# A four-layer residual stack on one core: where the gates of the third layer and its weighted candidate are made

## The chip, the cores and the metric

The kernel runs as one program on one core of a Trainium2 chip. The time is the device time of one execution in microseconds (us). The core has five engines, each with its own queue of instructions: TensorE (PE in the profile; PEld is its loading of weights), VectorE (DVE), ScalarE (ACT), GpSimd (POOL) and SyncE (SP, which here only issues DMAs). Engines wait for one another through semaphores. Products land in PSUM; everything else is in SBUF or in DRAM.

## The reference

The input is `x` with 32 rows of 256 steps of 256 features, and a condition vector per row. Four layers follow, each added to `x`. The first two are recurrences, the third is a scan, the fourth two matrix products per row.

```python
# layer 0, for each step t
z = sigmoid(x_t @ W_z + h @ U_z + vz); r = sigmoid(x_t @ W_r + h @ U_r + vr)
hh = tanh(x_t @ W + (r * h) @ U + vh); h = (1 - z) * h + z * hh
# layer 1, for each step t
gate = sigmoid(h1 @ Wh.T + z_t @ Wz.T + b); h1 = tanh(h1 * leak + gate * z_t)
# layer 2
f = sigmoid(x @ W_f.T + b_f); i = sigmoid(x @ W_i.T + b_i); s = f + i + EPS
new_info = (i / s) * (x @ W_h.T + b_h)
c = cumsum(log(f / s + EPS)); hidden = cumsum(exp(c[-1] - c_before) * new_info) + exp(c) * h0
# layer 3, with two matrices per row that are made of the condition vector
out = gelu(x @ down_row) @ up_row
```

In the kernel the candidate of layer 2 is `x @ W_h.T + b_h`, and its gates are `f` and `i`.

## The kernel before, in words

Features lie on the 128 partitions in two chunks (`NC` = 2, called `e` or `k`). All of `x` after layer 1 is kept in one SBUF tile, `X2`, of two chunks by 32 rows by 256 steps. The program has two parts.

**The recurrences** (the loop `for t in range(T + 1)`, 256 steps). Layers 0 and 1 run together, layer 1 one step behind. The batch of 32 is the stationary operand of TensorE (32 columns) and the weights stream past it. A weight matrix is cut into four quarters (`Q` = 4), and the four quarters run beside each other in four column strips of the array, 32 columns each, with `tile_position=(0, j * B)`. The helper `product` (its matmuls are line 528 in the profile) issues eight such matmuls: two chunks by four strips. Each fp32 matmul appears in the trace as two records of weight load and matmul. In one step TensorE does, in this order: `w_U_rz` times `hT` (the gates of layer 0), then whatever `products` holds for the step, then `w_l_Wz` (layer 1), `w_U_h` times `rhT`, `w_l_Wh` times `h1T`, and for the next step `w_W_rzh` times `x` (`project`, which in every second pair of steps first starts a new PSUM tile with the biases, `begin`, line 555). ScalarE makes `r` (line 655) and `z` (line 658, into the tile `keep`), the tanh of layer 1 (637), the tanh of layer 0 into `other` (697), layer 1's gate `gt` (706), and two scaled copies (708). VectorE multiplies `rh` in two halves (676), transposes it (604), combines `keep` (680), scans `h` in two halves (594), transposes that, and scans layer 1's `pre`.

`after(done, z_done)` makes the last matmul of the `w_l_Wz` product wait for `z`, so that the wait is already taken when `w_U_h` comes.

Side work is spread over the steps by dictionaries with a step as key (`transfers`, `products`, `moves`, `additions`, `sigmoids`, `sums`), which `due` empties at fixed places of the step. One kind of side work makes the matrices of layer 3 (`ada_weights`, `ada_matrix`, whose sums on VectorE are line 465). The other is the gates of layer 2, because a stretch of 32 steps (`CT`) can be worked on as soon as layer 1 has passed it. `gate_unit` takes one stretch, eight rows (`CB`) and one feature chunk: four matmuls of 128x128 weights by 256 columns (line 93), two for each gate, one per step; two sigmoids (115); a sum and a guard on VectorE (120, 123); three stores to DRAM (128). Six of the eight stretches (`NW_H` = 6) are done so: 48 units of four matmuls are 192 places. Ten of these places are second places in a step that already has one, every other step from 232 to 250 (`sorted(free + list(range(T - 24, T - 4, 2)))`).

**The turns** (the string `TURN`, run 10 times). Eight groups of four rows go through layers 2 and 3 as a pipeline of stages; a turn works on three groups at once at different stages, and `TURN` is the order in which the stages' instructions are issued to all engines. Per group: `fetch` brings the stored gates from DRAM (145); `late_gates` makes the last two stretches (matmuls at line 93 into `ps_g`, sigmoids 752 and 753, sums 759, 762); `candidate` makes `x @ W_h.T` for two rows and one chunk at a time (line 93 into `ps_c`, 512 columns) and `weigh` adds the bias and multiplies with `i` (777); `logs` (785); `sum_logs` (799); `exponents` (805); `exps` (810, 812); `scale_new` (817); `sum_new` (822); `add_first` (826); `add_hidden` adds to `X2` on GpSimd (833); then per row `middle` and `last`, each four matmuls of 128x128 by 256 columns (845), with a Gelu between them (858); `finish` adds `X2` on VectorE (867), stores the row, and loads the two matrices of the row four later (837).

## Time and profile before

| | |
|---|---|
| runs without a profile | 976.98, 979.28, 973.67 us; median 976.98 |
| the profiled execution | 977.23 us, of which the span from first to last instruction is 975.5 |
| mean granted TensorE clock | 0.993 |
| recurrences: first to last layer-1 tanh (line 637) | 21.1 to 758.4 us |
| one step in the middle of them | 2.86 us |
| turns: from there to the end of the span | 217.1 us |
| distance of equal places of neighbouring turns | 24.35 us |

How to read it: PE's busy time is an overlap of pipelined records, so that a full row of nines says little about how much more it could do. The useful readings are the times between starts of instructions that follow each other on one engine, the note in brackets (how long the engine was idle and who ended it), and the chain that ended last. In the recurrences every step has the same shape, so one step's timeline stands for them all; in the turns, one turn does.

### The profile page before, as it was taken

To read this page: it belongs to the slowest core of one execution; us is meant where nothing else is said; L and a number is where in the kernel's file an instruction comes from. 1 tells how busy PE (TensorE), PEld (TensorE's weight loads), DVE (VectorE), ACT (ScalarE), POOL (GpSimd) and SP (SyncE) were. 2 spreads that over 40 slices of the span, in tenths; PEclk is the share of its full clock that TensorE was granted. 3 is DMA by queue.
4 is the path that set the end of the run, shared out by engine and by line. 5 is a ranking of instruction groups with operands and counts; after the bars stand their busy time and mean duration, and the time that the engine had idled before them with its cause. 6 is when DMAs were issued, how large, how long until landed. Compare 5 with 4: busy or idle time off the path is not lost. (4 is left out here: it accounts for less than half of the span.)

```text
span 975.5 us, 54416 instructions
## 1 busy us (share of the span) xinstructions
PE 934.7 (96%) x22710; PEld 637.3 (65%) x22710; DVE 790.8 (81%) x3409; ACT 557.2 (57%) x2137; POOL 230.2 (24%) x594
## 2 busy tenths in 40 slices
PE   7999999999999999999999999999998889999978
PEld 3666666666666666666666666666665557777756
DVE  4766678888888888888888888888776599999995
ACT  3454455555555555555555555555554688888873
POOL 1233322222222222222222222222222022222222
PEclk9999999999999999999999999999999899999999
DMA  8245212222222222222222122222214747777643
GB/s 279 78 123 150 76 53 77 77 65 95 64 85 83 77 76 69 90 69 90 65 72 87 64 90 64 90 70 74 74 53 122 210 112 228 226 227 227 195 148 144
DMA packets 103577, 107.66 MB, mean 110 GB/s; under 512 B 9089, under 2 KB 86177, under 8 KB 103330
## 3 DMA queue, kind: packets, MB, share of 16 engines
q1 hardware_dynamic: 103330, 104.18, 34.1%
q8 instruction: 178, 2.92, 1.3%
q14 instruction: 69, 0.57, 0.2%
HBM read 59.06 MB, written 45.09 MB: 107 GB/s over the span
## 5 line engine op out<-in xcount | busy, mean ns | idle before, releaser
L528 PE MATMUL p<-w_W_rzh,xT 128*32 128x192 f32 x4096 | 216.3, 327 | 0.1
L594 DVE TENSOR_TENSOR_SCAN h<-other,keep 128x64 f32<-128x64 f32 x512 | 121.3, 279 | 75.2 <-ACT other L697 71.4
L528 PE MATMUL p<-w_U_rz,hT 128*32 128x128 f32 x4080 | 166.0, 279 | 10.5 <-issue 1.7
L697 ACT ACTIVATE other<-p 128x64 f32<-128x64 f32 x256 | 60.0, 234 | 196.4 <-PE p L528 196.4
L701 POOL TENSOR_TENSOR pairs<-xT,hT 128x64 f32<-128x64 f32 x256 | 82.3, 321 | 339.4 <-DVE other L717 280.8
L528 PEld LDWEIGHTS p<-w_U_rz,hT 128*32 128x32 f32 x4080 | 97.9, 108 | 93.5 <-DVE hT L604 90.6
L594 DVE TENSOR_TENSOR_SCAN pre<-other,pairs 128x128 f32<-128x128 f32 x256 | 123.3, 482 | 34.1 <-POOL pairs L701 0.2
L640 POOL TENSOR_TENSOR X<-pairs,h1T 128x64 f32<-128x64 f32 x256 | 96.6, 377 | 230.3 <-DVE rhT L604 226.9
L655 ACT ACTIVATE r<-p 128x64 f32<-128x64 f32 x255 | 57.0, 224 | 158.8 <-PE p L528 158.7
L528 PEld LDWEIGHTS p<-w_W_rzh,xT 128*32 128x32 f32 x4096 | 125.0, 110 | 23.1 <-issue 2.4
L708 ACT ACTIVATE pairs<-h1T,leak 128x32 f32<-128x32 f32 x510 | 133.7, 314 | 0.5
L528 PEld LDWEIGHTS p<-w_l_Wz,pairs 128*32 128x32 f32 x4096 | 77.3, 110 | 86.0 <-issue 70.9
L528 PE MATMUL p<-w_l_Wz,pairs 128*32 128x64 f32 x4096 | 119.6, 225 | 4.2 <-ACT keep L658 1.5
L528 PE MATMUL p<-w_U_h,rhT 128*32 128x64 f32 x4080 | 109.6, 225 | 2.0
L676 DVE TENSOR_TENSOR rh<-r,h 128x32 f32<-128x32 f32 x510 | 75.1, 189 | 41.2 <-ACT r L655 9.0
L528 PE MATMUL p<-w_l_Wh,h1T 128*32 128x64 f32 x4080 | 104.8, 220 | 0.5 <-issue 0.3
L604 DVE STREAM_TRANSPOSE hT<-h 128x32 f32<-128x32 f32 x512 | 84.2, 198 | 0.0
L833 POOL TENSOR_TENSOR X<-X,w 128x512 f32<-128x512 f32 x32 | 41.4, 1307 | 164.7 <-DVE w L826 76.8
L604 DVE STREAM_TRANSPOSE rhT<-rh 128x32 f32<-128x32 f32 x510 | 80.1, 195 | 0.0
L528 PEld LDWEIGHTS p<-w_l_Wh,h1T 128*32 128x32 f32 x4080 | 76.4, 110 | 0.5 <-ACT h1T L637 0.3
L528 PEld LDWEIGHTS p<-w_U_h,rhT 128*32 128x32 f32 x4080 | 69.1, 108 | 8.5 <-DVE rhT L604 8.5
L637 ACT ACTIVATE h1T<-pre 128x64 f32<-128x64 f32 x256 | 67.0, 262 | 1.4 <-DVE pre L594 1.4
(104 smaller groups left out, 1469.0 us busy)
## 6 DMA issues: line engine op xcount, KB each, us to landing
adapted<-wm SPq DMA_DIRECT2D x128, 128.0 KB
wt<-adapted SPq DMA_DIRECT2D x32, 512.0 KB
xT<-in_xT_dram SPq DMA_DIRECT2D x32, 256.0 KB
w<-in_W_dram SPq DMA_DIRECT2D x32, 256.0 KB
out_dram<-y SPq DMA_DIRECT2D x32, 256.0 KB
gates<-gate_i SPq DMA_DIRECT2D x48, 128.0 KB
gates<-gate_s SPq DMA_DIRECT2D x48, 128.0 KB
gates<-gate_g SPq DMA_DIRECT2D x48, 128.0 KB
```

The costliest lines, as they stand in the source:

```text
L528: last = nc.tensor.matmul(ps[j * B : (j + 1) * B, cols], hT[:, k, :], w[:, k, j, :], start=False, stop=False, skip_group_check=True, tile_ ...
L594: nc.vector.tensor_tensor_scan(*(x[:, ns].rearrange("p n u -> p (n u)") for x in (done, other, pairs)), 0.0, ALU.mult, ALU.add,)
L604: nc.vector.transpose(dst[:, c], src[:, bass.ts(c, B)])
L637: nc.scalar.activation(flat(h1T), pre, AF.Tanh)
L640: return nc.gpsimd.tensor_add(X2[:, :, :, s], by_chunk(pairs1.pop(s)[:, :, 0]), h1s.pop(s))
L655: nc.scalar.activation(r, p_0[t][:, cols_0(t, 0, 0)], AF.Sigmoid)
L676: rh_done = nc.vector.tensor_mul(rh[:, cs], r[:, cs], h[:, cs])
L697: nc.scalar.activation(other[:, :, 1], p_0[t][:, cols_0(t, 2, 2)], AF.Tanh)
L701: nc.gpsimd.tensor_add(by_chunk(pairs1[t][:, :, 0]), x_of(t), hT)
L708: nc.scalar.activation(by_chunk(pairs1[s][:, :, 1])[:, c], h1T[:, c], AF.Copy, scale=leak[:, c : c + 1],)
L833: after(nc.gpsimd.tensor_add(x, x, ws[g][:, b]), on_vector)
```

## The change

- **Units.** A unit of `gate_unit` now makes `f`, `i` and the candidate, each in one step: eight matmuls of 128x32 weights by 256 columns, in the four column strips, instead of two of 128x128 in two steps. Three PSUM results alternate between the two halves of `pg`. The candidate's bias and product with `i` (`weigh`) follow on VectorE one step later; `i` is stored after that. Seven stretches (`NW_H` = 7) are made so: 56 units of three places are 168 steps. There are no second places any more.
- **In the steps with such a place** (168; 147 of them where `changed` holds, all but those with `t % 8 == 2`) `w_l_Wz` comes behind `w_l_Wh`, and `gt` behind the two scaled copies. `after(done, z_done)` then puts the wait for `z` on the last of the eight new matmuls.
- **Halves.** `r` and the tanh of layer 0 are each made by two ACTIVATEs of 32 columns.
- **The turns.** `late_gates` makes one stretch with three products (128 columns each); `candidate` is gone; `weigh` has two instructions of 128 columns per group instead of four of 512. `add_hidden` is on VectorE. For three rows of four `X2` is added by TensorE (a matmul with the identity per chunk) and ScalarE copies `y` out. `TURN` has another order; `ps_l` has six buffers instead of four.
- **Transfers.** The matrices of the first four rows are loaded in halves from step 208 on, and the gates of group 0 in six pieces from step 238 on, instead of all after the last step. Chunks of `W2` and the matrices share one pool. The PSUM of the start has a pool of its own that is closed before the loop.

```diff
-NW_H = 6
+NW_H = 7
@@ gate_unit
-        def multiply(name, w, k):
-            gate_product(banks[name], w, e, k, slice(q * CB, (q + 1) * CB), h, h + 1)
+        def multiply(name, w, bank):
+            t["ps" + name] = bank
+            for k in range(NC):
+                for j in range(Q):
+                    js = slice(j * SQ, (j + 1) * SQ)
+                    done = nc.tensor.matmul(
+                        bank[js].rearrange("p (b t) -> p b t", t=CT),
+                        w[:, k, e * P + js.start : e * P + js.stop],
+                        X2[:, k, q * CB : (q + 1) * CB, h * CT : (h + 1) * CT],
...
+                        tile_position=(0, j * SQ),
+                    )
+            return done
+        def weigh():
+            nc.vector.scalar_tensor_tensor(
+                t["i"], t["psc"], vec("b_c", e), t["i"], ALU.add, ALU.mult
+            )
@@ the plan of the steps
-        free = sorted(free + list(range(T - 24, T - 4, 2)))
...
+                    for name, w in (("f", w_f), ("i", w_i), ("c", w_n)):
+                        t = free.pop(0)
+                        at(products, t, multiply, name, w, pg[:, len(units) % 2])
+                        units.add(t)
...
+        for n, (row, m) in enumerate((row, m) for row in range(GB) for m in range(2)):
+            at(transfers, T - 48 + 2 * n, load_matrices, row, slice(m, m + 1))
+        for n, (i, e) in enumerate((i, e) for i in (2, 0, 1) for e in range(NC)):
+            at(transfers, min(stored[0] + 2 + 2 * n, T), fetch_chunk, 0, i, e)
@@ the step
+        def by_halves(dst, src, function):
+            for c in range(NC):
+                nc.scalar.activation(dst[:, bass.ts(c, B)], src[:, bass.ts(c, B)], function)
...
-                        nc.scalar.activation(r, p_0[t][:, cols_0(t, 0, 0)], AF.Sigmoid)
+                        by_halves(r, p_0[t][:, cols_0(t, 0, 0)], AF.Sigmoid)
...
-                due(products, t)
+                done = due(products, t)
+                changed = t in units and t % U1 != U1_0
+                done = done[-1] if t in units else None
...
-                    done = product(p_1[s], cols_1(s), by_chunk(pairs1[s][:, :, 0]), w_1z)
+                    if not changed:
+                        done = with_wz()
                     if run0:
                         after(done, z_done)
...
                     product(p_1[s], cols_1(s), h1T, w_1h)
+                    if changed:
+                        with_wz()
...
-                    nc.scalar.activation(other[:, :, 1], p_0[t][:, cols_0(t, 2, 2)], AF.Tanh)
+                    by_halves(other[:, :, 1], p_0[t][:, cols_0(t, 2, 2)], AF.Tanh)
@@ the turns
+        for gate, w in enumerate((w_f, w_i, w_n)):
             for k in range(NC):
-                gate_product(ps[:, gate], w, e, k, slice(g * GB, (g + 1) * GB), NW_H, NH)
+                gate_product(ps[:, gate], w, e, k, slice(g * GB, (g + 1) * GB), NW_H)
...
+    BY_TENSOR = (1, 2, 3)
     def add_hidden(g, b):
-        after(nc.gpsimd.tensor_add(x, x, ws[g][:, b]), on_vector)
+        return nc.vector.tensor_add(x, x, ws[g][:, b])
...
+            if plus is not None:
+                nc.tensor.matmul(ps[:, e, :], ident, plus[:, e, :], start=False, stop=True)
...
+        if b in BY_TENSOR:
+            nc.scalar.copy(y, ys.pop(row))
```

The order of a turn after the change:

```
mid:1 new:2 new:3 sum:1.1 cum:3 cum:2 sum:0.1 sum:1.0 h0:2.1 sum:0.0 mid:0 h0:2.0
w:1 lf:1 w:0 h0:3.0 x:2 lf:0 last:1 exp:1 h0:3.1 sum:2.0 x:3 last:0 sum:3.1 in:2 y:1
sum:3.0 sum:2.1 exp:0 mid:2 w:3 w:2 ls:1 new:1 ls:0 y:0 cum:1 new:0 lg:1 h0:1.0
mid:3 last:2 h0:1.1 last:3 lg:0 cum:0 exp:3 m:1 x:1 exp:2 y:2 h0:0.1 ln:0 ln:1
h0:0.0 m:0 in:1 x:0 y:3 in:0
```

More of the change, by code (lines that the diff above doesn't have):

```diff
@@ L89, in load_gate_weights, with gate_product @@
         nc.sync.dma_start(out=w, in_=a[name].rearrange("(k p) e -> p k e", p=P))
-    def gate_product(ps, w, e, k, rows, h0, h1):
+    def gate_product(ps, w, e, k, rows, h):
         nc.tensor.matmul(
-            ps[:, 0 : (h1 - h0) * (rows.stop - rows.start) * CT].rearrange(
-                "p (h b t) -> p h b t", h=h1 - h0, t=CT
-            ),
+            ps.rearrange("p (b t) -> p b t", t=CT),
             w[:, k, e * P : (e + 1) * P],
-            X2[:, k, rows, h0 * CT : h1 * CT].rearrange("p b (h t) -> p h b t", t=CT),
+            X2[:, k, rows, h * CT : (h + 1) * CT],
             start=(k == 0),
@@ L101, in gate_product, with gate_unit @@
         )
-    def gate_unit(h, q, e, banks):
+    def gate_unit(h, q, e):
         t = {}
-        def multiply(name, w, k):
-            gate_product(banks[name], w, e, k, slice(q * CB, (q + 1) * CB), h, h + 1)
+        def multiply(name, w, bank):
[7 more added lines that the diff above has]
+                        X2[:, k, q * CB : (q + 1) * CB, h * CT : (h + 1) * CT],
+                        start=(k == 0),
+                        stop=(k == NC - 1),
+                        skip_group_check=True,
+                        tile_position=(0, j * SQ),
+                    )
+            return done
         def unit_tile(name):
@@ L115, in sigmoid @@
             nc.scalar.activation(
-                unit_tile(name), banks[name], AF.Sigmoid, bias=vec("b_" + name, e)
+                unit_tile(name), t["ps" + name], AF.Sigmoid, bias=vec("b_" + name, e)
             )
@@ L125, in guard, with fetch_chunk, fetch, load_matrices @@
             )
+        def weigh():
+            nc.vector.scalar_tensor_tensor(
+                t["i"], t["psc"], vec("b_c", e), t["i"], ALU.add, ALU.mult
+            )
         def store(name):
             nc.sync.dma_start(out=waiting[q][:, "gsi".index(name), e, h], in_=t[name])
-        return multiply, sigmoid, add_up, guard, store
+        return multiply, sigmoid, add_up, guard, weigh, store
     gi = ctx.enter_context(tc.tile_pool(name="gates_in", bufs=1))
     gated = {}
-    def fetch(g, i):
+    def fetch_chunk(g, i, e):
         name = "gsi"[i]
-        pool, bufs = (gp, 2) if i == 2 and g % 3 else (gi, 1)
-        tile_ = gated[name, g] = pool.tile(
-            [P, NC, NH, GB * CT], FP, name=f"in_{name}", tag=f"in_{name}", bufs=bufs
-        )
+        if e == 0:
+            pool, bufs = (gp, 2) if i == 2 and g % 3 else (gi, 1)
+            gated[name, g] = pool.tile(
+                [P, NC, NH, GB * CT], FP, name=f"in_{name}", tag=f"in_{name}", bufs=bufs
+            )
         q, half = divmod(g, CB // GB)
         cols = slice(half * GB * CT, (half + 1) * GB * CT)
+        nc.sync.dma_start(out=gated[name, g][:, e, 0:NW_H], in_=waiting[q][:, i, e, :, cols])
+    def fetch(g, i):
         for e in range(NC):
-            nc.sync.dma_start(out=tile_[:, e, 0:NW_H], in_=waiting[q][:, i, e, :, cols])
+            fetch_chunk(g, i, e)
+    am = ctx.enter_context(tc.tile_pool(name="matrices", bufs=4))
+    matrices = {}
+    def load_matrices(row, ms=slice(0, 2)):
+        if ms.start == 0:
+            matrices[row] = am.tile([P, 2 * NC * D], FP, name="wt", tag="wt").rearrange(
+                "p (m c d) -> p m c d", m=2, d=D
+            )
+        nc.sync.dma_start(
+            out=matrices[row][:, ms].rearrange("p m c d -> p m (c d)"),
+            in_=adapted[row // GB][row % GB, :, ms],
+        )
     with ExitStack() as rec:
@@ L153 @@
         pa = rec.enter_context(tc.tile_pool(name="rec_pa", bufs=2, space=PSUM))
-        px = rec.enter_context(tc.tile_pool(name="aux_ps", bufs=1, space=PSUM))
+        ahead = ExitStack()
+        ph_pool = ahead.enter_context(tc.tile_pool(name="ahead_ps", bufs=1, space=PSUM))
         U0, U1 = 2, 8
@@ L162, in four_banks @@
             return px.tile([P, Q, 512], FP, name=name, tag="px")
-        pg = px.tile([P, 2, CB * CT], FP, name="pg", tag="pg")
         def chunk_tile(name):
-            return ax.tile([P, NC, Q, CH], FP, name=name, tag="w2")
+            return [
+                am.tile([P, Q * CH], FP, name=name, tag="wt").rearrange("p (j n) -> p j n", j=Q)
+                for k in range(NC)
+            ]
         def weights(name, g):
@@ L227 @@
             load_row(a["bias_rows"])
-            w_c = chunk_tile("w_c")[:, :, :, 0 : 3 * S]
+            w_c = [w[:, :, 0 : 3 * S] for w in chunk_tile("w_c")]
             for k in range(NC):
                 nc.sync.dma_start(
-                    out=w_c[:, k], in_=a["C_rzh"][k * P : (k + 1) * P]
+                    out=w_c[k], in_=a["C_rzh"][k * P : (k + 1) * P]
                 )
@@ L293, in rows_into @@
                     )
-            ahead = four_banks("ahead")
-            halves = [ahead[:, half] for half in range(2)]
+            halves = [ph_pool.tile([P, 512], FP, name=f"pv_{half}") for half in range(2)]
             for half in range(2):
                 rows_into(halves[half], 2 * half)
-            pt, ph = (
-                ahead[:, bank, 0 : NC * B].rearrange("p (c b) -> p c b", b=B) for bank in (2, 3)
-            )
+            pt, ph = (ph_pool.tile([P, NC, B], FP, name=name) for name in ("pt", "ph"))
             for k in range(NC):
@@ L313 @@
                             condT[:, k, :],
-                            w_c[:, k, hs, :],
+                            w_c[k][:, hs, :],
                             start=False,
@@ L342 @@
             nc.scalar.preload_act_table_set("sigmoid_and_others")
+            ahead.close()
+        px = rec.enter_context(tc.tile_pool(name="aux_ps", bufs=1, space=PSUM))
+        pg = px.tile([P, 2, CB * CT], FP, name="pg", tag="pg")
         for t, (f, *args) in (
@@ L374, in load @@
                 nc.sync.dma_start(
-                    out=tiles["w2"][:, k, hs],
+                    out=tiles["w2"][k][:, hs],
                     in_=a["W2"][:, k, at_col : at_col + 2 * CH].rearrange(
@@ L395, in multiply @@
                         hyT[:, k, :],
-                        tiles["w2"][:, k, j, :],
+                        tiles["w2"][k][:, j, :],
                         start=(k == 0),
@@ L499 @@
         free = [t for t in range(CT + 3, T) if t not in products]
-        free = sorted(free + list(range(T - 24, T - 4, 2)))
+        units = set()
+        stored = {}
         for h in range(NW_H):
@@ L505 @@
                         free.pop(0)
-                    multiply, sigmoid, add_up, guard, store = gate_unit(
-                        h, q, e, {"f": pg[:, 0], "i": pg[:, 1]}
-                    )
-                    for name, w in (("f", w_f), ("i", w_i)):
-                        for k in range(NC):
-                            t = free.pop(0)
-                            at(products, t, multiply, name, w, k)
-                        at(sigmoids, t, sigmoid, name)
-                    at(sums, t + 1, add_up)
-                    at(sums, t + 2, guard)
-                    for n, name in enumerate("isg"):
-                        at(transfers, t + 2 + n // 2 + (n == 2), store, name)
+                    multiply, sigmoid, add_up, guard, weigh, store = gate_unit(h, q, e)
+                    for name, w in (("f", w_f), ("i", w_i), ("c", w_n)):
+                        t = free.pop(0)
+                        at(products, t, multiply, name, w, pg[:, len(units) % 2])
+                        units.add(t)
+                        if name != "c":
+                            at(sigmoids, t, sigmoid, name)
+                        if name == "i":
+                            at(sums, t + 1, add_up)
+                            at(transfers, t + 2, store, "s")
+                    at(sums, t + 1, weigh)
+                    at(sums, t + 2, guard)
+                    stored[q] = t + 3
+                    for name in "ig":
+                        at(transfers, t + 2 + (name == "g"), store, name)
+        for n, (row, m) in enumerate((row, m) for row in range(GB) for m in range(2)):
+            at(transfers, T - 48 + 2 * n, load_matrices, row, slice(m, m + 1))
+        for n, (i, e) in enumerate((i, e) for i in (2, 0, 1) for e in range(NC)):
+            at(transfers, min(stored[0] + 2 + 2 * n, T), fetch_chunk, 0, i, e)
         assert max(*transfers, *products, *moves, *additions, *sums) <= T
@@ L662, with with_wz @@
                 due(moves, t)
-                due(products, t)
+                done = due(products, t)
+                changed = t in units and t % U1 != U1_0
+                done = done[-1] if t in units else None
+                def with_wz():
+                    return product(p_1[s], cols_1(s), by_chunk(pairs1[s][:, :, 0]), w_1z)
                 if run1:
@@ L705, with gate_1 @@
                     gt = sp.tile([P, S], FP, name="gt", tag="gt")
-                    nc.scalar.activation(gt, p_1[s][:, cols_1(s)], AF.Sigmoid)
+                    def gate_1():
+                        nc.scalar.activation(gt, p_1[s][:, cols_1(s)], AF.Sigmoid)
+                    if not changed:
+                        gate_1()
                     for c in range(NC):
@@ L711 @@
                         )
+                    if changed:
+                        gate_1()
                     if t % U1 == U1_0 and run0:
@@ L718 @@
                     late = s, multiply_add("pre", other, pairs1[s])
-            for g, i in ((0, 2), (0, 0), (0, 1)):
-                fetch(g, i)
             finish_1()
@@ L741 @@
     fs, ss, ccs, ws, pcs, parts_f = {}, {}, {}, {}, {}, {}
-    matrices, mids, ys = {}, {}, {}
-    LATE = slice(NW_H, NH)
+    mids, ys = {}, {}
     def late_gates(g, e):
-        ps = pp.tile([P, 2, 256], FP, name="ps_g", tag="ps_g")
-        for gate, w in enumerate((w_f, w_i)):
+        ps = pp.tile([P, 4, GB * CT], FP, name="ps_g", tag="ps_g")
+        for gate, w in enumerate((w_f, w_i, w_n)):
             for k in range(NC):
-                gate_product(ps[:, gate], w, e, k, slice(g * GB, (g + 1) * GB), NW_H, NH)
-        dst = parts_f[g, e] = gu.tile([P, 256], FP, name="gate_f", tag="gate_f")
+                gate_product(ps[:, gate], w, e, k, slice(g * GB, (g + 1) * GB), NW_H)
+        dst = parts_f[g, e] = gu.tile([P, GB * CT], FP, name="gate_f", tag="gate_f")
+        pcs[g, e] = ps[:, 2]
         nc.scalar.activation(dst, ps[:, 0], AF.Sigmoid, bias=vec("b_f", e))
@@ L755, in late @@
     def late(g, name, e):
-        return gated[name, g][:, e, LATE].rearrange("p h n -> p (h n)")
+        return gated[name, g][:, e, NW_H]
     def late_sum(g, e):
@@ L764, in late_guard, with weigh @@
         )
-    def candidate(g, u):
-        r, e = divmod(u, NC)
-        b0 = g * GB + r * 2
-        ps = pp.tile([P, 512], FP, name="ps_c", tag="ps_c")
-        pcs[g, u] = ps.rearrange("p (h n) -> p h n", h=NH)
-        for k in range(NC):
-            gate_product(ps, w_n, e, k, slice(b0, b0 + 2), 0, NH)
-    def weigh(g, u):
-        r, e = divmod(u, NC)
-        m = gated["i", g][:, e, :, r * 2 * CT : (r + 1) * 2 * CT]
+    def weigh(g, e):
+        m = late(g, "i", e)
         return nc.vector.scalar_tensor_tensor(
-            m, pcs.pop((g, u)), vec("b_c", e), m, ALU.add, ALU.mult
+            m, pcs.pop((g, e)), vec("b_c", e), m, ALU.add, ALU.mult
         )
@@ L828, in add_first, with times @@
         )
+    BY_TENSOR = (1, 2, 3)
     def add_hidden(g, b):
         x = X2[:, :, g * GB + b, :]
-        after(nc.gpsimd.tensor_add(x, x, ws[g][:, b]), on_vector)
-    def load_matrices(row):
-        wt = matrices[row] = ap.tile([P, 2, NC, D], FP, name="wt", tag="wt")
-        nc.sync.dma_start(
-            out=wt.rearrange("p m c d -> p m (c d)"), in_=adapted[row // GB][row % GB]
-        )
-    def times(row, m, src):
-        ps = pp.tile([P, NC, T], FP, name="ps_l3", tag="ps_l3", bufs=4)
+        return nc.vector.tensor_add(x, x, ws[g][:, b])
+    def times(row, m, src, plus=None):
+        ps = pp.tile([P, NC, T], FP, name="ps_l3", tag="ps_l3", bufs=6)
         for e in range(NC):
@@ L849, in times @@
                     start=(k == 0),
-                    stop=(k == NC - 1),
+                    stop=(k == NC - 1 and plus is None),
                 )
+            if plus is not None:
+                nc.tensor.matmul(ps[:, e, :], ident, plus[:, e, :], start=False, stop=True)
         return ps
@@ L861, in last @@
         row = g * GB + b
-        ys[row] = times(row, 1, mids.pop(row))
+        x = X2[:, :, row, :]
+        ys[row] = times(row, 1, mids.pop(row), x if b in BY_TENSOR else None)
     def finish(g, b):
@@ L866, in finish @@
         y = ap.tile([P, NC, T], FP, name="y", tag="y")
-        done = nc.vector.tensor_add(y, ys.pop(row), X2[:, :, row, :])
+        if b in BY_TENSOR:
+            nc.scalar.copy(y, ys.pop(row))
+            done = None
+        else:
+            done = nc.vector.tensor_add(y, ys.pop(row), X2[:, :, row, :])
         nc.sync.dma_start(out=out[:, row], in_=y)
@@ L875 @@
         "lf": (late_gates, 0), "ls": (late_sum, 0), "lg": (late_guard, 0),
-        "c": (candidate, 0), "m": (weigh, 0), "ln": (logs, 0), "in": (fetch, -1),
+        "m": (weigh, 0), "ln": (logs, 0), "in": (fetch, -1),
         "sum": (sum_logs, 1), "w": (exponents, 1), "exp": (exps, 1),
@@ L882 @@
     TURN = """
-        lf:0 new:2 new:3 cum:2 sum:0.0 mid:1 in:2 mid:0 sum:1.0 cum:3 h0:2.0 lf:1 sum:0.1
-        sum:3.1 last:1 sum:1.1 sum:3.0 w:1 exp:1 h0:3.1 h0:2.1 w:0 ls:0 h0:3.0 ls:1 c:0
-        sum:2.0 w:3 lg:0 lg:1 x:2 m:0 y:1 x:3 exp:0 last:0 c:1 m:1 exp:3 c:3 y:0 mid:2 mid:3
-        new:1 sum:2.1 new:0 w:2 cum:0 cum:1 c:2 h0:0.1 h0:0.0 exp:2 ln:1 h0:1.1 h0:1.0 ln:0
-        last:2 x:1 m:3 last:3 y:2 in:1 x:0 m:2 in:0 y:3
+        mid:1 new:2 new:3 sum:1.1 cum:3 cum:2 sum:0.1 sum:1.0 h0:2.1 sum:0.0 mid:0 h0:2.0
[3 more added lines that the diff above has]
+        h0:0.0 m:0 in:1 x:0 y:3 in:0
     """
     with tc.manual_schedule():
-        for row in range(GB):
-            load_matrices(row)
-        tables, on_vector = False, None
+        tables = False
         for turn in range(NG + 2):
@@ L910 @@
                     tables = False
-                on_vector = f(g, *args) or on_vector
+                f(g, *args)
 def _laid_out(v):
```

## The prediction

> **What bounds the kernel now.** I read the page's busy line, then the chain that ended last, then one step's and one turn's timeline.

> ```profile
> PE 934.7 (96%) x22710; PEld 637.3 (65%) x22710; DVE 790.8 (81%) x3409; ACT 557.2 (57%) x2137; POOL 230.2 (24%) x594
> ```

> PE's 96% is an overlap of records and misleads in the recurrences. There a step of 2.86 us is one loop through four engines. From the timeline, the step that begins at 502.91:

> ```profile
> 502.91 0.64 PE L528 MATMUL p<-w_U_rz,hT 128*32 128x128 f32 x16
> ...
> 503.48 0.70 PE L93 MATMUL pg<-X,w_W_f 128*128 128x256 f32 x2
> 503.62 0.22 ACT L655 ACTIVATE r<-p 128x64 f32<-128x64 f32 x1 [0.74 <-PE p L528]
> 503.74 0.22 ACT L658 ACTIVATE keep<-p 128x64 f32<-128x64 f32 x1
> ...
> 503.88 0.29 DVE L676 TENSOR_TENSOR rh<-r,h 128x32 f32<-128x32 f32 x2
> 504.10 0.31 DVE L604 STREAM_TRANSPOSE rhT<-rh 128x32 f32<-128x32 f32 x2
> 504.11 0.27 PEld L528 LDWEIGHTS p<-w_l_Wz,pairs 128*32 128x32 f32 x16 [0.33 <-issue]
> ...
> 504.37 0.27 PEld L528 LDWEIGHTS p<-w_U_h,rhT 128*32 128x32 f32 x16
> ...
> 504.87 0.24 ACT L697 ACTIVATE other<-p 128x64 f32<-128x64 f32 x1 [0.76 <-PE p L528]
> ...
> 505.13 0.47 DVE L594 TENSOR_TENSOR_SCAN h<-other,keep 128x64 f32<-128x64 f32 x2
> ...
> 505.52 0.33 DVE L604 STREAM_TRANSPOSE hT<-h 128x32 f32<-128x32 f32 x2
> ...
> 505.76 0.38 PEld L528 LDWEIGHTS p<-w_U_rz,hT 128*32 128x32 f32 x16 [0.30 <-DVE hT L604]
> ```

> Counted from `w_U_rz`: `r` 0.71, `z` 0.83 to 1.05, `rh` 0.97, `rhT` 1.19, `w_U_h` 1.46, tanh 1.96, scan 2.22, `hT` 2.61, next step 2.86. The gate product ends before `rhT` is there, so it is hidden. Two lines carry the forecast. In a step with little on PE, the last matmul of `w_l_Wz`, which waits for `z`, stands alone 0.5 us after the other seven:

> ```profile
> 62.40 0.26 PEld L528 LDWEIGHTS p<-w_l_Wz,pairs 128*32 128x32 f32 x14 [0.23 <-POOL pairs L701]
> ...
> 62.90 0.14 PEld L528 LDWEIGHTS p<-w_l_Wz,pairs 128*32 128x32 f32 x2 [0.24 <-ACT keep L658]
> ```

> That is 0.05 us after `z` ended. And in the ten doubled steps PE is late:

> ```profile
> 723.39 1.13 PE L93 MATMUL pg<-X,w_W_i 128*128 128x256 f32 x4
> ...
> 724.45 0.43 PE L528 MATMUL p<-w_l_Wz,pairs 128*32 128x64 f32 x16
> 724.64 0.30 PEld L528 LDWEIGHTS p<-w_U_h,rhT 128*32 128x32 f32 x16
> ```

> `w_U_h` starts 1.89 us into the step instead of 1.46, and the step takes 3.26: what PE delays there, the step pays in full.

> In the turns PE and DVE are both full. The windows view and the chain:

> ```profile
> 827.00:852.00 25.00, 25.00 (x98) 18.41 (x98) 24.41 (x43) 22.38 (x32) 5.79 (x6) 1.00 0.73 224
> ```

> ```profile
> 813.42 1.73 PE ps_g L93 x8
> ...
> 837.78 1.73 PE ps_g L93 x8
> ```

> Columns of the first: PE, PEld, DVE, ACT, POOL busy, clock, DMA share, GB/s. A turn is 837.78 - 813.42 = 24.36 us. Start to start, PE needs 16 x 0.216 for `ps_g`, 16 x 0.43 for `ps_c`, 64 x 0.216 for `ps_l`: 24.1. DVE: `cc` 8 x 0.587, `sum_new` 4 x 1.125, `h0` 8 x 0.39, `new` 4 x 0.60, `weigh` 4 x 0.66, `y` and `w` 8 x 0.59, late sums and guards 4 x 0.34: 23.4.

> **The change, part by part.**

> *Gate steps.* Eight column-strip matmuls of 256 columns. Records of 64, 128, 192 and 256 columns take 219, 273, 327 and 379 ns, so a pass streams in 0.21 us, and a strip has four: 0.85 us. Without any wait that ends 0.48 + 0.85 = 1.33 us into the step, before `rhT`: hidden. But the eighth matmul now waits for `z`. `r` in two halves takes ACT 2 x 0.09 us (the 64-column ACTIVATE starts its successor after 0.12, less 0.03 for half the columns) instead of 0.12, so `z` ends at 1.11 and PE sees it at 1.17. Only then may strip 3 begin its second chunk: 0.24 + 0.21, ready at 1.62. `w_U_h` could have started at 1.43 (`rh` 0.03 earlier) and cannot finish in strip 3 before the 1.62 is over. Behind it are queued, on the same strip, `w_U_h`, `w_l_Wh` and now `w_l_Wz` (0.22 each, 504.62 to 504.84), in every second pair of steps `begin` (0.16, 63.72 to 63.88) and `w_W_rzh` (0.65), and ACT waits for all of them. Counted from `r`:

> - through PE alone: `z` seen 0.45, strip 3 done 0.90, three products 1.56, `begin` 1.72, `w_W_rzh` 2.37, `w_U_rz` to `r` 0.67: 3.04 us a step where `begin` stands (86 of the 147 changed steps, counted from the plan);
> - through `hT`, without `begin` (61): 0.90, last group of `w_U_h` to tanh 0.46, to scan 0.23, to `hT` 0.39, to PE 0.24, to `r` 0.71: 2.93 us.

> So 86 x 0.18 + 61 x 0.07 = +20 us. Bounds: below nothing (-0.07 a step if the wait is not felt) and the doubled step's +0.40. I take the walk, which lies nearest to the row at 62.90. The 21 other gate steps keep `w_l_Wz` ahead of `w_U_h`: gate to 1.33, `w_l_Wz` to 1.55, +0.05 each: +1.

> *Halves.* In the 88 steps without a place, `rh` and the scan can start 0.03 us earlier each: 88 x 0.06 = -5; nothing, where VectorE's side sums end just ahead of the scan (they do at 505.13), -6 at most. [...]

> *Doubled steps* gone: 10 x 0.40 = -4.

> *End of the recurrences.* PE idles 1.67 us at 747 while six gate loads run at once, and the granted clock is 0.5 from 749.8 to 753.3. Loads spread over 48 steps may avoid it: -1 (0 to -3). SP only issues them (0.3 us each).

> Recurrences: +20 + 1 - 5 - 4 - 1 = **+11 us**.

> *Turns.* PE: `lf` has 24 records of 128 columns; the 128x32 record with full weights starts its successor after 0.112, so 2.7; `mid` 6.9; `last` 6.9 plus 12 identity records, 2.6: 19.1. DVE loses three `y`, three quarters of `weigh`, 40% of the late sums, and gains four additions at the price of `new`: 4.7 + 4.5 + 3.1 + 2.4 + 0.5 + 0.6 + 2.4 + 0.8 + 2.4 = 21.4. ACT: five table loads of 1.29, `exps` 4 x 1.47, logs 4 x 1.04, Gelu 2.0, sigmoids 1.0, three copies at 0.55: 21.2. DVE and ACT end last now, PE not. The DMA share rises from 0.73 by 7% more bytes in 10% less time to 0.87; a turn's lead covers that. Two full engines that wait for each other will not reach 21.4; PE as the one bound reached 24.36 of 24.1. I take 21.9 (21.4 to 23.5).

> From 788.9 (first `mid`) to 935.0 are six turns: 146.1 - 131.4 = -15. The filling (758.4 to 788.9) loses `ps_c`'s 7 us of PE, but its logs (4.2) and table loads stay: -4 (0 to -7). The last two turns gain 5 us of PE work for the identities and lose three GpSimd additions of 1.3 on the chain: +1 (-2 to +3). Turns: **-18 us**. The first 21 us stay.

> Sum: 977.2 + 11 - 18 = **970 us**, against the profiled execution's own 977.23 (span 975.5 and 1.7 around it); the median, 976.98, is the same within 0.03%.

> **Rivals.**

> - *A: the wait for `z` isn't felt.* If strip 3 catches up, a changed step is 2.86 with `begin` and 2.79 without: -4 in place of +20. 977 - 13 - 18 = 946. For it: the records show strips running independently. Against it: 62.90.
> - *B: the turns don't shorten*, since ACT and DVE hand rows back and forth: 23.5 us a turn, -5 in place of -15: 980. For it: ACT was busy 22.4 of 25 us already. Against it: its work shrinks.
> - *C: slower, by the eighth matmul's wait in the 147 changed steps.* If the late strip also holds back the matmuls dispatched behind it, so that a step costs +0.26 (between the walk's 0.135 and the doubled step's 0.40), that is 38 in place of 20: 988. It decides from +0.22 a step (slower by over 0.5%), and undoes the rest from +0.18.
> - That the change doesn't move the work is excluded: the built order has eight `pg` matmuls per place and no `ps_c`.

> **Numbers.** Half a per cent (4.9 us) is what a measurement of this kernel can tell from no change. Chances: forecast 0.50 (960 to 982; of it 0.36 faster, 0.12 same, 0.02 slower), A 0.20 (faster), B 0.14 (0.10 same, 0.04 slower), C 0.16 (slower). Faster 0.56, same 0.22, slower 0.22. The range takes in A and C: 944 to 988.

> **What would show it.** In a changed step the last two `pg` weight loads stand alone, ended by ACT `keep`, about 1.17 us in; steps of 3.04 and 2.93 in pairs; plain steps at 2.79; no idle PE near the last steps; turns of 21.9 with DVE over 95% busy and PE under 90%. Changed steps at 2.86 or less, or above 3.1, or turns above 23, prove a step wrong.

## The result, and the profile after

The changed kernel took 967.08 us (median of 5 runs, 966.26 to 970.26) against 976.98: a ratio of 0.9905, 95% interval 0.9876 to 0.9934. The forecast was 970. The profiled execution took 968.89 us with a span of 967.1, that is 8.3 us less than the 977.23 of before. The page's busy line, and under it the chain that ended last by engine:

```profile
PE 915.1 (95%) x25046; PEld 700.1 (72%) x25046; DVE 802.8 (83%) x3473; ACT 571.5 (59%) x2682; POOL 195.3 (20%) x562
...
DVE 9%; PE 5%; ACT 3%; DMA 1%; issue 1%; DVEq 0%; ACTq 0%
```

PE has 2336 records of each kind more than before and is busy for less time; as the prediction said, that share decides nothing. Both parts have to be read by their own clocks.

**The recurrences.** The weight loads of a changed step without `begin`, from the timeline (start, duration, engine and line, operation; in brackets the idle time before it and who ended it):

```profile
501.49 0.38 PEld L575 LDWEIGHTS p<-w_U_rz,hT 128*32 128x32 f32 x16 [0.18 <-DVE hT L651]
501.85 0.66 PEld L112 LDWEIGHTS pg<-X,w_W_f 128*32 128x32 f32 x14
502.67 0.14 PEld L112 LDWEIGHTS pg<-X,w_W_f 128*32 128x32 f32 x2 [0.15 <-ACT keep L709]
502.93 0.31 PEld L575 LDWEIGHTS p<-w_U_h,rhT 128*32 128x32 f32 x14
503.13 0.16 PEld L575 LDWEIGHTS p<-w_l_Wh,h1T 128*32 128x32 f32 x4
503.18 0.11 PEld L575 LDWEIGHTS p<-w_U_h,rhT 128*32 128x32 f32 x1
...
503.24 0.11 PEld L575 LDWEIGHTS p<-w_U_h,rhT 128*32 128x32 f32 x1
...
504.41 0.38 PEld L575 LDWEIGHTS p<-w_U_rz,hT 128*32 128x32 f32 x16 [0.18 <-DVE hT L651]
```

Fourteen loads of the gate product run through; the last two, those of the eighth matmul, stand alone at 502.67, 1.18 us into the step, and `keep`, which is `z`, ended their wait. The last two loads of `w_U_h` come at 503.18 and 503.24, after the loads of `w_l_Wh` have begun: what the late strip holds up is its own work, and the other strips go on. The step is 504.41 - 501.49 = 2.92 us long.

To see all steps, I took the distance from one `r` to the next for each of the 254 pairs of neighbouring steps in the trace and sorted them by what the plan puts into the step. "Long" is what all steps together take above the medians of their own kinds (a step under its median counts against it).

| us | plain (86) | gates, `w_l_Wz` ahead (21) | changed, no `begin` (61) | changed, `begin` (86) | long, sum | first to last `r` |
|---|---|---|---|---|---|---|
| before | 2.856 | 2.858 | 2.856 | 2.857 | 9.7 | 735.3 |
| after | 2.801 | 2.886 | 2.918 | 3.036 | 12.0 | 752.6 |

The columns of before are the same steps `t`, whatever they hold there.

**The turns.** One turn in the windows view (us, then busy time of PE, PEld, DVE, ACT, POOL, the granted clock, DMA share, GB/s):

```profile
832.86:854.28 21.42, 19.78 (x100) 17.03 (x100) 21.42 (x41) 21.10 (x33) 0.11 (x1) 1.00 0.88 275
```

VectorE is never idle, ScalarE hardly, and TensorE has 1.6 us left (it is 92% busy, where the prediction asked for under 90%). VectorE's instructions recur every 21.43 us, the Gelus of ScalarE every 21.57; before, a turn took 24.35.

From before to after by these stretches: the first `r` comes at 15.2 us and not at 18.0 (-2.8); the recurrences take 17.3 us more; the rest of the span, 222.2 us before, takes 199.3 (-22.9).

### The profile page after: what moved, and what is told of

It reads as the page before. It is cut to its first block, busy times and chain, and to the rows that moved or that the text cites. A ratio compares the mean times of both kernels' runs of the same rounds, so it can differ in the third digit from the quotient of the medians.

```text
span 967.1 us, 59663 instructions
## 1 busy us (share of the span) xinstructions
PE 915.1 (95%) x25046; PEld 700.1 (72%) x25046; DVE 802.8 (83%) x3473; ACT 571.5 (59%) x2682; POOL 195.3 (20%) x562
## 5 line engine op out<-in xcount | busy, mean ns | idle before, releaser
L659 ACT ACTIVATE other<-p 128x32 f32<-128x32 f32 x512 | 74.7, 200 | 189.9 <-PE p L575 189.9
L659 ACT ACTIVATE r<-p 128x32 f32<-128x32 f32 x510 | 72.8, 195 | 166.8 <-PE p L575 166.8
L575 PE MATMUL p<-w_l_Wz,pairs 128*32 128x64 f32 x4096 | 142.2, 221 | 8.6 <-ACT keep L709 2.8
L575 PEld LDWEIGHTS p<-w_l_Wz,pairs 128*32 128x32 f32 x4096 | 106.0, 110 | 40.0 <-ACT keep L709 12.7
L575 PE MATMUL p<-w_U_h,rhT 128*32 128x64 f32 x4080 | 130.9, 223 | 0.1
L575 PE MATMUL p<-w_l_Wh,h1T 128*32 128x64 f32 x4080 | 126.8, 219 | 1.2 <-ACT other L659 0.6
L575 PEld LDWEIGHTS p<-w_U_h,rhT 128*32 128x32 f32 x4080 | 91.9, 108 | 25.4 <-DVE rhT L651 0.6
L575 PEld LDWEIGHTS p<-w_l_Wh,h1T 128*32 128x32 f32 x4080 | 97.5, 109 | 1.8 <-ACT other L659 0.7
L899 PE MATMUL ps_l<-mid,wt 128*128 128x256 f32 x256 | 66.7, 389 | 12.2 <-ACT mid L914 12.1
L112 PE MATMUL pg<-X,w_W_c 128*32 128x256 f32 x896 | 76.6, 381 | 0.0
```

Source lines behind the costliest of these rows:

```text
L112: done = nc.tensor.matmul(bank[js].rearrange("p (b t) -> p b t", t=CT), w[:, k, e * P + js.start : e * P + js.stop], X2[:, k, q * CB : (q ...
L575: last = nc.tensor.matmul(ps[j * B : (j + 1) * B, cols], hT[:, k, :], w[:, k, j, :], start=False, stop=False, skip_group_check=True, tile_ ...
L659: nc.scalar.activation(dst[:, bass.ts(c, B)], src[:, bass.ts(c, B)], function)
L899: nc.tensor.matmul(ps[:, e, :], matrices[row][:, m, k, e * P : (e + 1) * P], src[:, k, :], start=(k == 0), stop=(k == NC - 1 and plus is N ...
```

## Experiments

Step kinds are written plain / gates with `w_l_Wz` ahead / changed without / changed with `begin`. Times are medians; ratios are to before, run on the same chip. Experiments 1 to 4 ran on one chip, 5 to 8 on a second, 9 to 11 on a third and 12 on a fourth. Steps and long steps are read from the profiled execution.

**1. The wait left off the gate product.**

```diff
-                    if run0:
+                    if run0 and not changed:
                         after(done, z_done)
```

> The early wait for z is no longer put on the eighth gate matmul of the 147 changed steps; the wait then falls on the first w_U_h matmul, which also waits for rhT, so the built order has one more waiting instruction of TensorE's queue there. Theory (the wait holds column strip 3 and with it everything behind it): changed steps fall from 3.04 to about 2.86 where begin stands (86) and from 2.92 to about 2.79 where not (61), -23 us, less what one more waiting instruction after rhT costs (0.06 us a step would give back 9): 944 to 953 us. Rival (TensorE is simply full in these steps, with or without the wait): steps stay at 3.04 and 2.92, 967 us.

998.61 us, ratio 1.0213 (1.0184 to 1.0242): neither side foresaw it. The wait doesn't vanish: `w_U_h` needs `keep`'s semaphore anyhow, and the built program gives it a waiting instruction of its own, for `rhT`, ahead of the matmul that waits for `z` (TensorE has 284 such instructions in this trace, 137 in the changed kernel's). Steps 2.807 / 2.890 / 2.884 / 3.128, so the wait's price did fall in the steps without `begin` (from 2.918). In those with `begin` the step grew from 3.036: in the median `w_U_h` starts 0.78 us after `r` in place of 0.72, and `w_W_rzh`, the last product of the step, 1.54 in place of 1.42. And the long steps rose from 12.0 to 37.2 us. Of TensorE's waits between 25 and 745 us, in the changed kernel and here (line, cause, us in total, times, longest):

```profile
PE p L575 <- issue: 2.9, 7, 0.6
```

```profile
PE p L575 <- issue: 16.0, 34, 1.3
```

"issue" is time in which nothing that the profile shows held TensorE. That was the first sign of a cost that no theory had.

**2. `w_l_Wz` ahead of the wait in all gate steps.**

```diff
-                changed = t in units and t % U1 != U1_0
+                changed = False
```

> w_l_Wz and gt keep their old places in all 168 gate steps, and the early wait is on the last w_l_Wz matmul again; the eight gate matmuls stay. Theory: all gate steps become like the 21 that kept the order, 2.89 us, so 147 x (2.89 - 2.99) = -15 us: 952 us. Rival (TensorE is full, and w_l_Wz ahead of w_U_h delays w_U_h by its 0.22 us): changed steps at 3.1 to 3.2, 980 to 1000 us.

962.82 us, ratio 0.9849 (0.9825 to 0.9874). Steps 2.802 / 2.888 / 2.887 / 2.892: in the medians 86 x 0.144 + 61 x 0.031 = 14.3 us are won, about what theory asked for, but only 5.7 arrive, since the long steps rise from 12.0 to 20.4 us.

**3. Only a quarter of the eighth matmul waits.**

```diff
-                    done = nc.tensor.matmul(
-                        bank[js].rearrange("p (b t) -> p b t", t=CT),
+                    cuts = (0, CB - 2, CB) if k == NC - 1 and j == Q - 1 else (0, CB)
+                    for b0, b1 in zip(cuts, cuts[1:]):
+                        done = nc.tensor.matmul(
+                            bank[js].rearrange("p (b t) -> p b t", t=CT)[:, b0:b1],
```

> The eighth gate matmul is cut into 192 and 64 columns, and only the 64-column piece carries the wait for z. Same work for TensorE but for one more weight load. Theory: the piece runs from 1.21 to 1.34 us into the step, before rhT at 1.43, so the wait costs nothing: changed steps 2.86 and 2.79, 944 us. Rival (TensorE is full): 3.04 and 2.92 or a little more, 967 us or above.

971.31 us (ten runs, nine from 966.77 to 974.53 and one at 981.68), ratio 0.9941 (0.9924 to 0.9958): by the time alone, theory fell. By the steps it holds where no `begin` stands: 2.803 / 2.894 / 2.801 / 2.918, that is 2.80 for the 2.79 it asked. Where `begin` stands, 2.918 is two thirds of the way from 3.04 to 2.86; the rest stays, so there the wait is not all of the price. Each kind of changed step is shorter by 0.118 us, in all 17.3 us, and the trace shows where: in the steps without `begin` the last load of `w_U_h` comes 0.88 us after `r` in place of 1.03, and the tanh 1.22 in place of 1.34 (medians). The long steps give it all back: 29.7 us in place of 12.0, and the unchanged steps are among them. One such step in the timeline:

```profile
729.65 0.36 PEld L577 LDWEIGHTS p<-w_U_rz,hT 128*32 128x32 f32 x10 [0.26 <-DVE hT L653]
...
731.50 0.12 PEld L577 LDWEIGHTS p<-w_U_rz,hT 128*32 128x32 f32 x3 [1.50 <-issue]
...
731.98 0.28 ACT L661 ACTIVATE r<-p 128x32 f32<-128x32 f32 x2 [2.33 <-PE p L577]
```

TensorE stops after ten of the sixteen loads of one product, whose operands are all there, and stands for 1.5 us. In the trace's packet records a 16 KB instruction packet starts at 729.10, and TensorE goes on 2.40 us later. So it is in 19 of this run's 20 stops in the recurrences (over 0.55 us from one record's start to the next): they end 2.2 to 3.2 us after the start of an instruction packet, a stretch that covers a quarter of the time. In the changed kernel 8 of 9 do. The 19 steps with such a stop make up 15.8 of the 29.7 us; what makes the others long is not shown.

**4. `r` and the tanh whole again.**

```diff
-                        by_halves(r, p_0[t][:, cols_0(t, 0, 0)], AF.Sigmoid)
+                        nc.scalar.activation(r, p_0[t][:, cols_0(t, 0, 0)], AF.Sigmoid)
...
-                    by_halves(other[:, :, 1], p_0[t][:, cols_0(t, 2, 2)], AF.Tanh)
+                    nc.scalar.activation(other[:, :, 1], p_0[t][:, cols_0(t, 2, 2)], AF.Tanh)
```

> r and the tanh of layer 0 are one ACTIVATE of 64 columns each again. Theory: the 108 steps without a changed place lose 0.06 us (2.80 to 2.86, +6 us), but z comes 0.06 us earlier, so that the changed steps gain 0.06 where begin stands and 0.03 where not (-7 us): 966 us, no difference. Rival (halves help in every step alike): +0.06 in all 255 steps, 982 us.

969.97 us, ratio 0.9918 (0.9892 to 0.9944), not told apart from the changed kernel. Steps 2.858 / 2.921 / 2.889 / 2.975: the halves win 0.057 us in each plain step (4.9) and 0.035 in the 21 (0.7), and cost 0.029 and 0.061 in the changed ones (1.8 + 5.2), where the second half puts `z` off (it starts 0.17 us after `r` and not 0.12). By the medians they cost 1.4 us, too little for the runs to show.

**5 to 7. What brings the instruction packets late?** All three build on either the cut of experiment 3 or the changed kernel. In experiment 3 the DMA engines had been busy for 0.53 of the 1.5 us before a packet that a stop followed (0.30 before the other packets), so their traffic was the suspect. In the first, `store` sends only stretch 0, and `fetch_chunk` reads that stretch seven times:

```diff
+            if h == 0:
                 nc.sync.dma_start(out=waiting[q][:, "gsi".index(name), e, h], in_=t[name])
```

> The gate matmul that waits for z is cut as in the run before it (192 + 64 columns), and the gates of the first stretch alone are stored (24 of 168 transfers of 128 KB); the turns read that stretch's gates seven times, so the cumulative gates are not the reference's. Theory now: the cut took 0.12 us from each of the 147 changed steps in the median (3.04 to 2.92, 2.92 to 2.80), and the 18 us so won were lost again to long steps (30 us above the medians of their kinds against 12 in the changed kernel), in which TensorE stands for want of instructions: its 16 KB instruction packets come late where the DMA engines are busy (they were busy 0.52 of the 1.5 us before a packet with a stall, 0.30 before the others). With six in seven of the stores gone, the time above the medians should fall from 30 to 10 to 18 us and the time to 950 to 960. Rival: the stalls come from TensorE's own rate, whatever the DMA engines do; then time above the medians stays near 30 and the time near 968 to 971.

968.43 us, ratio 0.9907 (0.9886 to 0.9927); steps 2.804 / 2.888 / 2.800 / 2.918 and long steps 27.7 us: the rival's result. But the stops of over 0.55 us fell from 20 to 13, so some did go with the stores. The second adds to the changed kernel

```diff
+            nc.sync.dma_start(out=again[q][:, "gsi".index(name), e, h], in_=t[name])
```

> The changed kernel with every one of its 168 gate stores issued twice, the second time to another place in DRAM. Theory (late instruction packets): the medians of the steps stay at 3.04, 2.92 and 2.80, the time above the medians rises from 12 to 25 us or more, and the time to 975 to 990. Rival (TensorE's own rate): no more than 2 us either way, 965 to 969.

976.31 us, ratio 0.9976 (0.9958 to 0.9993); 2.805 / 2.889 / 2.920 / 3.038, long steps 19.9 us: the medians stay and the long steps grow by 8, as theory says, though by less than it asked. Against experiment 8, which leaves the recurrences of the changed kernel as they are and has 14.3 us of long steps on the same chip, they grow by 5.6. The third cuts each store by partitions (`waiting[q][js, ...]`, `js` 64 of 128 partitions) and sends the second half a step later:

> The cut of 192 + 64 columns, with each gate store halved by partitions and the halves sent in two steps one after the other (336 transfers of 64 KB). Theory (late instruction packets): a packet now waits behind half as much, the time above the medians falls from 30 to about 20 us, and the time to 958 to 965. Rival (TensorE's own rate, or the total of bytes and not their lumps): 967 to 971.

979.65 us, ratio 1.0026 (0.9999 to 1.0052), long steps 40.4 us and 3.039 in the 21 unchanged gate steps, over half of which are long here: worse than either side said (the profiled execution was at 984.26). Doubled stores went with 5.6 to 8 us more of long steps, but with six sevenths of them gone 27.7 of 29.7 us were left. As the main cause traffic fell; why halved stores make more of it stays open.

**8. y's additions back on VectorE.**

```diff
-    BY_TENSOR = (1, 2, 3)
+    BY_TENSOR = ()
```

> The changed kernel with y's additions for all four rows given back to VectorE (no row by TensorE); all else stays. Theory: VectorE sets the turns, 21.4 us of work in a turn of 21.43; its sum rises to about 23.2, so each of seven turns takes 1.8 us more: turns of 23.2, time 978 to 981. Rival: ScalarE (21.2 in a turn, here less) and the order of the work set them; then turns stay under 22 and the time under 971.

978.74 us, ratio 1.001 (0.9995 to 1.0024). VectorE's instructions recur every 23.22 us, and a turn reads

```profile
834.60:857.80 23.20, 18.72 (x85) 15.93 (x85) 23.20 (x43) 18.88 (x28) 0.11 (x1) 0.85 0.86 262
```

ScalarE has 4 us to spare here, TensorE as much, and the turn still takes what VectorE's work takes. The granted clock of 0.85 is not the cause: in the turn before it is 1.00, and VectorE's instructions recur at the same 23.22. This part of the change is worth 1.8 us a turn. That the time lies in the expected range owes something to chance, though: of the 11.7 us between the two profiled spans 9.2 lie behind the recurrences, and 2.8 in them, where the edit changes nothing.

**9. Half a packet more in front.** On the cut of experiment 3, ahead of the first step:

```diff
+            for _ in range(32):
+                nc.tensor.matmul(
+                    pg[0:SQ, 0, 0:1], condT[:, 0, :], condT[:, 0, 0:1],
+                    start=True, stop=True, skip_group_check=True, tile_position=(0, 0),
+                )
             project(0)
```

> The cut of 192 + 64 columns (967.8 us, 29.7 us above the medians), and 32 matmuls of one column more before the first step (128 TensorE records, half of a 16 KB instruction packet; their result is written over later). Theory: where a step becomes long is set by where in it an instruction packet ends, so that the same kernel with 24 stores or with halved stores has its long steps at the same places (t = 48, 57, 73, 82, 95, 153, 157, 161, 178, 182, 218). With the stream moved by half a packet most of these go and others come, and the sum above the medians stays between 20 and 40 us; time 960 to 980. Rival: the steps are long for what else is done in them (transfers, ScalarE's or VectorE's extra work); then the long steps stay where they were.

961.62 us, ratio 0.9867 (0.9827 to 0.9907), though the first `r` comes 4.4 us later for the added matmuls. Medians 2.799 / 2.887 / 2.801 / 2.917, long steps 14.8 us in place of 29.7, under the 20 to 40 that theory gave (the profiled execution, 957.58, is the fastest of four). TensorE's waits between 25 and 745 us, without and with the added matmuls:

```profile
PE p L577 <- issue: 11.1, 21, 1.2
```

```profile
PE p L577 <- issue: 5.4, 15, 0.8
```

And the places moved. Of the steps from t = 11 on that lie over 0.25 us above their median, the cut has 43, and shares 19 with the run with few stores (5 would be chance) and 30 with the run of halved stores (10 by chance): three kernels with one and the same stream of TensorE instructions and other traffic. With this run, which has other boundaries and the same traffic, it shares 1 of 20 (3 or 4 by chance). Another chip alone doesn't move the places so: the stream of experiment 2 on this chip (experiment 10) shares 6 of its 15 with experiment 2's 29 (2 by chance). So the place of the packet boundaries in the step has a large part in where TensorE stops. How much of the fall from 29.7 to 14.8 us is theirs stays open, since the chip is another one and that stream, too, has half its long steps here.

**10. The sum in the turns by GpSimd** (on experiment 2):

```diff
-        return nc.vector.tensor_add(x, x, ws[g][:, b])
+        nc.gpsimd.tensor_add(x, x, ws[g][:, b])
```

> w_l_Wz ahead of the wait in all gate steps (962.8 us, turns of 21.56), and in the turns the addition x + w for each row by GpSimd instead of VectorE. Theory (VectorE's sum sets the turn, as y's additions given back showed: 23.22 for 21.43): VectorE's sum falls by about 2.4 to 19, ScalarE is next with some 21.2, so turns of 21.2 and a time 2 to 4 us lower, 959 to 961. Rival: GpSimd's addition is on the way of each row to its multiplication and is several times VectorE's in length, or slows VectorE while it runs; then turns are longer than 21.6 and the time over 965.

963.03 us, ratio 0.9861 (0.9826 to 0.9895), and turns of 22.84 instead of 21.56: the rival, by the turns (it asked for a time over 965). The turn and one group of VectorE in it, then the same group in experiment 2 (busy us, mean ns):

```profile
828.84:851.70 22.86, 20.01 (x101) 16.79 (x100) 22.86 (x36) 22.00 (x33) 7.45 (x6) 1.00 0.84 259
```

```profile
L884 DVE SCALAR_TENSOR_TENSOR w<-cc,condT,w 128x256 f32<-128x256 f32 x16 | 10.5, 685 | 0.0
```

```profile
L884 DVE SCALAR_TENSOR_TENSOR w<-cc,condT,w 128x256 f32<-128x256 f32 x16 | 7.3, 475 | 0.0
```

VectorE lost 5.4 us of additions in two turns and got longer instructions for it: 475 became 685 ns in the mean. Those that a GpSimd addition overlaps took 1.18 to 1.50 us, all others 0.45 to 0.48: that is the rival's second way, VectorE slowed while GpSimd runs. The total stayed at 963, since the rest of the span took 10.2 us more, but the long steps were 10.4 us in place of experiment 2's 20.4, with the same stream of TensorE instructions in the recurrences, on another chip.

**11. Each kind of step its own order.** The 86 steps with `begin` take `w_l_Wz` ahead of the wait, the 61 others the cut:

```diff
+        def held(t):
+            return t in units and t % U1 != U1_0 and (t + 1) // 2 % U0 != 0
...
-                    cuts = (0, CB - 2, CB) if k == NC - 1 and j == Q - 1 else (0, CB)
+                    cuts = (0, CB - 2, CB) if cut and k == NC - 1 and j == Q - 1 else (0, CB)
...
-                changed = t in units and t % U1 != U1_0
+                changed = held(t)
```

> The 86 changed steps that have a begin take w_l_Wz ahead of the wait (2.89 us in the median), the 61 others take the cut of 192 + 64 columns (2.80). By the medians the steps are 5 us shorter than with w_l_Wz ahead everywhere (746.9). Theory (late instruction packets take a good part back): steps between 740 and 750, time 956 to 964.

950.09 us, ratio 0.9736 (0.9715 to 0.9757): the fastest here, 17 us under the changed kernel and under the 956 to 964 that was expected. Steps 2.801 / 2.888 / 2.800 / 2.888, long steps 13.9 us. Of the 19.9 us that the medians give (86 x 0.148 + 61 x 0.118), 18.0 arrive. TensorE's waits on "issue" in the step products, between 25 and 745 us, sum to 4.8 us here (ten of them) and to 11.1 in experiment 3 (21).

**12. The changed kernel with half a packet more in front** (the edit of experiment 9):

> The changed kernel itself (967.1 us, steps 752.6, of them 12.0 above the medians) with the same 32 small matmuls before the first step. Theory (long steps are where an instruction packet ends at the wrong place): medians stay at 3.04, 2.92, 2.89 and 2.80, the long steps move, and their sum changes by chance to anything from 5 to 25 us: time 958 to 982, and few of the long steps at t = 52, 60, 84, 147, 223, 239, 240, 247 stay. It tells how much of the measured time is the placing of packets. Rival (the long steps belong to what those steps do): the same places and a time of 966 to 970.

972.1 us, ratio 0.9949 (0.9929 to 0.9969). The first `r` is 4.1 us later, the recurrences take 752.0 (752.6), the medians are 2.801 / 2.889 / 2.922 / 3.036, and the long steps sum to 11.1 us (12.0) at other places: of the eight that were named none is among them. So in one other position the sum is the same: nothing here says that the changed kernel owes its time to lucky boundaries.

## Why the prediction was right

- **Gate steps, +20 and +1.** The medians give 86 x 0.179 + 61 x 0.062 = 19.2 and 21 x 0.028 = 0.6. The walk's 3.04 and 2.93 were 3.036 and 2.918. Experiments 2 and 3 show the cause: with a shorter piece behind the wait, or more work ahead of it, the same steps fall by 0.118 and 0.03 to 0.144 us. In the steps with `begin` the wait is 0.118 of the 0.179; the other 0.06 stays in experiment 3, where little waits. That fits the walk's first path, through TensorE's own queue, but no run takes it apart. Rival A had the right floor (2.80 without `begin`), but the wait is felt; rival C didn't come.
- **Halves, -5.** 86 x 0.055 = 4.7 in the plain steps, 2.80 for the forecast 2.79. Over all steps they cost 1.4 us (experiment 4); their price in the changed steps is inside the +20. The halves' own row:

```profile
L659 ACT ACTIVATE r<-p 128x32 f32<-128x32 f32 x510 | 72.8, 195 | 166.8 <-PE p L575 166.8
```

  195 ns, 29 less than the 224 of 64 columns before, and the second one starts some 0.09 us after the first (a pair takes 0.28). The sum that was worked from rows of 64 columns held.
- **Doubled steps and the end, -5.** This is the term that was wrong. What the last 32 steps take above their medians fell from 6.8 to 3.1 us (-3.7), and the stall at 747 went. But that stall was of the kind of experiment 3: in the kernel before an instruction packet starts at 746.03, and TensorE stops after ten matmul records of a product and goes on 2.72 us later. The prediction named only the loads that ran then.

```profile
746.46 0.63 PE L528 MATMUL p<-w_U_rz,hT 128*32 128x128 f32 x10
748.75 0.31 PE L528 MATMUL p<-w_U_rz,hT 128*32 128x128 f32 x3 [1.67 <-issue]
```

  So the forecast had no long steps elsewhere, and the other 223 steps took 9 us above their medians in place of 3. "No idle PE" was wrong for that reason: TensorE stands in single steps all along (nine stops of 0.57 to 0.90 us in the changed kernel's recurrences). The recurrences came to +17.3 instead of +11.
- **Turns, -18.** Six turns took 131.0 us by the Gelus instead of 146.2: -15.2 for -15. The forecast 21.9 a turn is 21.57 from the second turn on, and 23.1 in the first. VectorE's sum of 21.4 was exact. The two full engines hardly lose anything to one another, so rival B is out. The filling, at -4 (0 to -7), measured -6.9, near its bound. The last two turns measured -0.8 for +1.
- **"The first 21 us stay."** They were 2.8 us shorter in this one profile. In the kernels here that leave the start as it is, the first `r` came at 14.7 to 17.6 us, so single executions differ by as much, and one profile can't say whether the change did it.

The errors of the parts (+6 in the recurrences, -5 in the turns, -3 at the start) took each other off, and that was luck: against the profiled execution the sum was off by 1 us, less than any of them.

Open: how much of experiment 1's loss is packets, how much its extra waiting instruction; and why one and the same stream has 29.7, 27.7 and 40.4 us of long steps with different stores (experiments 3, 5 and 7), and 20.4 and 10.4 where only the turns and the chip differ (2 and 10): the place of the boundaries alone doesn't account for these sums. Experiment 3's stream in another position was tried once, not in a sweep.

## What to carry to other kernels

Put a wait that must be taken early on the smallest piece of work that still does it (here 0.118 us a changed step, experiment 3), and put the work that doesn't need it ahead (0.031 and 0.144 us, experiment 2). Compare steps by the median of their kind, and what lies above the medians by itself: a gain that the time doesn't show may be there in every step and lost in a few (in experiment 3, 17.3 us by the medians and 17.7 more in the long steps). The order that is best by the medians still has to be run: by them experiment 3 won more than experiment 2 (17.3 us, 14.3), and its time was the longer one (971.31, 962.82); with 128 TensorE records more in front, only 1 of 20 long steps stood where the cut of experiment 3 has one (experiment 9).
